# A graph layer on one core: later copies of counts and chunk sums, 560 counted chunks in passes of 30 units, four sets of one-hots

## The chip, the cores and the metric

The kernel runs on one core of a Trainium2 chip. The metric is the device time of one execution in microseconds (us). Engines are named as the profile names them: PE (TensorE, the matmuls), PEld (its weight loads), DVE (VectorE), ACT (ScalarE), POOL (GpSimd, here the issuer of gathers) and SP (SyncE, here an issuer of transfers).

## The reference

```python
h = jnp.maximum(_layernorm(x, axis=-1), 0.0)          # x: 12500 nodes x 128
xs = h[src]                                           # 200,000 edges, sorted by dst
for i in range(4):                                    # four types of edge
    msgs = msgs + jnp.where((edge_type == i)[:, None], xs @ W[i] + b[i], 0.0)
out = x + jax.ops.segment_sum(msgs, dst, num_segments=12500)
```

The edges are drawn so that low node numbers get many of them: node 0 and its neighbours are the target of very many edges, the last nodes of few.

## The kernel before, in words

First the normalized table h is written to DRAM (htab), each number in three 16-bit parts (one f16, two bf16), 384 values a row. The 200,000 sorted edges are cut into 1563 chunks of 128. They are dealt with in two ways.

**Counted chunks.** The first C0 = 568 chunks lead to the nodes with many edges. For these the kernel does not fetch rows. It counts, for each target node, how often each pair of source node and edge type occurs, and multiplies the counts with the whole table. Up to three target nodes share one 32-bit number, one byte each; such a packed group is a *unit*. The edges of a unit lie in one or more *slots* of up to 128 edges. `count` (from L1030) makes two one-hots per slot on DVE: o2 (128x392, L1049) and o1 (128x128, L1057). One matmul per slot (L1075) adds their product to the unit's bank of PSUM, `pt`, of which the pool `x_ps` has four. After the unit's last slot ACT copies the bank as integers into `counts` (L1081). The one-hots are made in sets of SLOTS = 4 slots. There are SETS = 3 sets of buffers: a set's buffers are written again when the set three before has been counted, and the loop (L1062 to L1069) keeps two sets made or in the making ahead of the one that is counted. The same pool `x_ps` also serves a bank for the weights of a group (`pc`, L646), the transposes of the results (`leave`, L750, called by `put_out`), those of the preparation (`prep_steps`) and the product with W (L1190).

A batch is up to UB = 31 units; there are 19 batches, the first of 22 units and 18 of 31, thus 580 units in 1069 slots. `multiply` (L1112 on) takes a counted batch through all 98 blocks of 128 table rows, fetched three blocks at a time (hs, 288 KB, SP). For each block PE does two matmuls (L1172) into one bank `pa`: the f16 part with the counts read as fp8 digits, and the second part in fp32r with digits that ACT has decoded (`dec`, L1130, three blocks at a time, 128 x 3 x 372, DECS = 4 buffers; three of them are decoded when the batch starts). The first batch does three fp8 matmuls instead and writes a table of two parts (dtab) for the rest. At the end ACT copies `pa` out (sd, L1186), `tail` multiplies it with W (L1190), and DVE adds it up (L1209).

After a batch has been counted, `check_sums` (L1086 to L1106) looks on DVE whether the sums hold. Its first step, `bi` (L1089), reads the last row of all counts of the batch, so it needs the batch's last copy. It is a list of steps of which the main loop takes one per part (L1508).

**Gathered chunks.** The other 995 chunks go in groups of 16 (the last groups have 8, 12, 8, 4 and 3, so 65 groups). POOL gathers one row of htab per edge (hm, L589, two chunks to a buffer, ten buffers). DVE makes one-hots of the target window (oh, L607). `sum_up` does three matmuls per chunk (L625) into `ps`, a pool `s_ps` of two banks of four chunks (SG = 4); after four chunks ACT moves the sums out (sb, L631). `weigh` brings the sums times W into `py` (L653, L655), `ring_adds` adds them to a ring (L718), and the results leave by `put_out`. The first RAW = 3 groups are read from x itself, 48 gathers of L573.

**Order.** On PE, DVE and ACT instructions run in the order in which the program emits them. The main loop (L1476 on) goes through the groups; `sum_up` hands back after each part of two chunks, and then the loop takes as much of the counted side as `pace` (L1222) says. `dense_work` (L1237) yields in turn steps of `count` of the next batch and of `multiply` of the last, by columns, with a lead of BEHIND = 0.15 for the counting, so that the counting of a batch ends before the product of the one before does. From group FULL-1 = 59 on, `pace` wants all counted work done; what is left then is 35 gathered chunks (8, 12, 8, 4 and 3), the tail. The program's one wait on the counted side between batches is by data: the first decodes (L1130) of a batch stand on ACT right behind the sd of the batch before, and the copies of the next batch's counts behind them.

Of the kernel before, what the change touches and what calls it, by code (L numbers as in the profile page):

```python
# [35 lines left out]
F32 = mybir.dt.float32  # L36
# [7 lines left out]
AF = mybir.ActivationFunctionType  # L44
# [6 lines left out]
P = 128  # L51
EPS = 1e-5
UN = 3
G = 16
SG = 4
WIN = 32
ROOM = 6
C0 = 568
UB = 31
MANY = 16  # L60
HB = 3
SLOTS = 4
ODDS = 5
SETS = 3
STREAM = 5
BEHIND = 0.15
SETTLE = 0.5
RING = 1024
OT = 4
HG = 2  # L70
# [12 lines left out]
def kernel(  # L83
# [26 lines left out]
    BM = -(-TM // P)  # L110
    BR = 16
    BC = -(-TM // BR)
    assert C0 % 8 == 0 and C0 <= NFULL


    q = E0 / E
# [226 lines left out]
    def prep_steps(m, prep):  # L343
# [22 lines left out]
        nc.vector.tensor_sub(ends[:, m : m + 1, 0], ends[:, m : m + 1, 0], span[:, m : m + 1])  # L366
        nc.vector.tensor_reduce(ends[:, m : m + 1, 1], rel, AX.X, ALU.min)
        yield 1
        pg = x_ps.tile([P, 2, P], F32, name="pt")
        nc.tensor.transpose(pg[:, 0, :], sf[:, 0, :], ident)  # L370
        nc.tensor.transpose(pg[:, 1, :], key[:, 0, :], ident)
# [229 lines left out]
    def one_hots_of(t0, g):  # L601
# [6 lines left out]

        return oh, [lambda i=i: make(i) for i in range(g)]

    adds = []
    finish = []
    flushing = []

    def sum_up(t0, g, rows, oh, last):
        win = window_of(C0 + t0)
        K = NT * win
        sb = []
        finish.append(weigh(t0, g, oh, sb, last))
        for i0 in range(0, g, SG):  # L620
            i1 = min(i0 + SG, g)
            ps = s_ps.tile([P, 512], F32, name="ps")[:, : SG * K].rearrange("p (i n) -> p i n", i=SG)
            for i in range(i0, i1):
                for c in range(3):
                    nc.tensor.matmul(ps[:, i - i0, :], rows(i, c), oh[:, i, :], start=(c == 0), stop=(c == 2))  # L625
                if i % HG and i + 1 < i1:
                    yield (i + 1) / g
            if i0 == 0:
                to = spool.tile([P, G * KM], F32, name="sb", bufs=1)[:, : G * K]
                sb.append(to.rearrange("p (g t n) -> p g t n", g=G, t=NT))  # L630
            nc.scalar.activation(  # L631
                sb[0][:, i0:i1].rearrange("p g t n -> p g (t n)"), ps[:, : i1 - i0, :], AF.Copy, scale=1.0 / UP
            )
            yield i1 / g

    def weigh(t0, g, oh, sb, last):
        win = window_of(C0 + t0)

        def bank(own):
            to = y_ps.tile([P, G * WIN], F32, name="py") if own else x_ps.tile([P, G * WIN], F32, name="pt")  # L640
            return to[:, : G * win].rearrange("p (g n) -> p g n", g=G)

# [383 lines left out]
    def count(vs, counts):  # L1026
# [34 lines left out]
        made = []  # L1061
        done = 0  # L1062
        for n, of in enumerate(sets):
            while len(making) < min(n + 3, len(sets)):
                making.append(make(len(making)))
                made.append([])
            for m in range(n, min(n + 2, len(sets))):
                made[m] += list(making[m])
            for k, (i, s, by, first, last) in enumerate(of):  # L1069
                if n + 2 < len(sets) and len(made[n + 2]) < len(sets[n + 2]):  # L1070
                    made[n + 2].append(next(making[n + 2]))
                o1, o2, _ = made[n][k]
                if first:
                    pb = x_ps.tile([P, NB + NT], F32, name="pt")
# [3 lines left out]
                if k == len(of) - 1:  # L1078
                    released[before + n] = one.ins
                if last:  # L1080
                    nc.scalar.copy(counts[:, :, i * NT : (i + 1) * NT], pb.rearrange("p (b t) -> p b t", t=NT))  # L1081
                done += 1
                yield done / len(todo)
            made[n] = None

        def check_sums():  # L1086
            n = len(vs)
            bi = sdp.tile([P, UB], I32, name="bi")
            nc.vector.tensor_copy(bi[:, :n], counts[:, NW, : n * NT].rearrange("p (i t) -> p i t", t=NT)[:, :, 0])  # L1089
            yield True  # L1090
# [22 lines left out]
    def multiply(vs, counts):  # L1113
# [71 lines left out]
        sd = sdp.tile([P, 3 * UB * NT], F32, name="sd")  # L1185
        nc.scalar.activation(sd[:, :nv], pa[:, :nv], AF.Copy, scale=512.0 / UP)  # L1186
        def tail():
            py = x_ps.tile([P, 3 * UB], F32, name="pt")
            for t in range(NT):
                nc.tensor.matmul(  # L1190
# [285 lines left out]
    for gi, (t0, g) in list(enumerate(zip(starts, sizes)))[RAW:]:  # L1476
# [20 lines left out]
        for j, part in enumerate(sum_up(t0, g, *now, gi >= FULL)):  # L1497
# [204 lines left out]
```

## Time and profile before

| what | value |
|---|---|
| median of 3 runs | 1642.27 us |
| the three runs | 1640.22, 1642.27, 1651.68 us |
| the profiled execution | 1648.93 us |
| its span, first to last instruction | 1647.2 us |
| mean granted clock of PE | 0.909 of full |
| instructions | 30145 |

How to read it: in a row of groups, the line of the kernel, the engine and the operation come first, then what is written and read with its shape, the number of instructions, the busy time of all, the mean of one in ns, and the idle time of that engine just in front of them with the one that ended most of it. "issue" is a time in front of which nothing in the profile was waited for. In a row of waits the three numbers are the total in us, how many times, and the longest. In a row of the timeline stand the start, the time from first to last, the engine, the line and the operation, and in brackets the idle time before. In a row of windows stand the stretch, its length, the busy time of PE, PEld, DVE, ACT and POOL with their instruction counts, the granted clock of PE, the share of the DMA engines and GB/s.

### The profile page before, as it was taken

What the parts mean: (1) busy time and instruction counts of PE and PEld (TensorE: products, weight loads), DVE (VectorE), ACT (ScalarE), POOL (GpSimd) and SP (SyncE); (2) the same over time, 40 slices, a digit from 0 to 9 for tenths busy, and PEclk for the clock granted to TensorE, in tenths of its full rate; (3) what the DMA queues carried; (4) which work ended last, traced back from release to release, by engine and by line L of the source; (5) the groups of instructions that cost most, each with busy time, mean ns of one, the idle gap of its engine ahead of it and who ended that gap; (6) DMA issues with size and microseconds to landing.
All of it is one profiled execution on the core that took longest, in us unless ns stands there. A gap on an engine that the chain in (4) does not pass through costs nothing.

```text
span 1647.2 us, 30145 instructions
## 1 busy us (share of the span) xinstructions
PE 1345.8 (82%) x9232; PEld 902.9 (55%) x9232; DVE 999.9 (61%) x5139; ACT 1082.6 (66%) x1815; POOL 970.2 (59%) x1024
## 2 busy tenths in 40 slices
PE   4876878888888888798878879788879888797965
PEld 1344655565655555465655556555656655565644
DVE  7785559466666657666554756456554746564523
ACT  5676446676767677677767677677767767666621
POOL 6535444656656565656656665566656666656563
PEclk9785897989999898998999999999989999999977
DMA  7542695766766676767766676576767676667842
GB/s 215 168 170 67 206 335 162 237 185 205 210 190 207 185 224 176 217 186 211 210 196 208 205 214 203 172 215 199 211 186 213 190 220 197 191 177 219 254 120 75
DMA packets 184628, 322.54 MB, mean 196 GB/s; under 512 B 30243, under 2 KB 82524, under 8 KB 184460
## 3 DMA queue, kind: packets, MB, share of 16 engines
q1 hardware_dynamic: 132716, 214.63, 42.1%
q0 software_dynamic: 46992, 96.30, 20.9%
q10 hardware_dynamic: 4752, 9.64, 1.5%
q8 instruction: 73, 1.20, 0.3%
q14 instruction: 95, 0.78, 0.1%
HBM read 294.78 MB, written 25.67 MB: 195 GB/s over the span
## 4 chain that ended last, share of the span: by engine, by line
PE 65%; issue 11%; ACT 9%; DVE 8%; DMA 3%; another core or an unknown queue 3%; POOL 0%; SPq 0%; DVEq 0%; ACTq 0%
PE pa L1172 33%; PE pt L1075 12%; PE py L655 7%; PE ps L625 6%; ACT dec L1130 4%; DVE o L1057 2%; DVE o L1049 2%; PE pt L1190 2%; DVE ring L718 1%; ACT counts L1081 1%; DMA hs<-htab 1%; DMA hs<-dtab 1%; PE pt L646 1%; PE pt L936 1%
## 5 line engine op out<-in xcount | busy, mean ns | idle before, releaser
L589 POOL DMA_INDIRECT hm<-htab,srcT x947 | 918.0, 969 | 616.8 <-issue 217.2
L1130 ACT ACTIVATE dec<-counts 128x1116 fp32r<-128x1116 uint8 (+1 forms) x594 | 663.2, 1137 | 23.9 <-remote 13.7
L1049 DVE TENSOR_SCALAR o<-iota_n,hkT 128x392 bf16<-128x392 f16 x1069 | 351.8, 329 | 300.6 <-PE pt L1075 172.9
L1172 PE MATMUL pa<-dec,hs 128*128 128x372 f32 x1764 | 498.5, 389 | 30.6 <-issue 19.8
L1172 PE MATMUL pa<-counts,hs 128*128 128x372 fp8e4 (+1 forms) x2058 | 449.7, 330 | 48.0 <-issue 22.8
L1075 PE MATMUL pt<-o,o 128*128 128x396 bf16 x1069 | 308.9, 359 | 98.0 <-issue 37.7
L1172 PEld LDWEIGHTS pa<-dec,hs 128*128 128x128 f32 x1764 | 317.9, 195 | 99.5 <-issue 44.3
L1081 ACT CAST counts<-pt 128x396 int32<-128x396 f32 x580 | 272.5, 496 | 148.2 <-PE pt L1075 55.7
L1172 PEld LDWEIGHTS <-hs 128*128 128x128 f16 (+1 forms) x2058 | 191.1, 99 | 191.7 <-issue 73.2
L631 ACT ACTIVATE sb<-ps 128x288 f32<-128x288 f32 (+8 forms) x237 | 98.3, 415 | 238.6 <-PE ps L625 76.0
L1057 DVE TENSOR_SCALAR o<-iota,loT,byT 128x128 bf16<-128x128 bf16 x647 | 213.8, 330 | 0.0
L625 PE MATMUL ps<-oh,hm 128*128 128x72 bf16 (+7 forms) x2841 | 185.8, 202 | 32.7 <-issue 25.9
L625 PEld LDWEIGHTS <-hm 128*128 128x128 f16 x2841 | 139.2, 101 | 97.6 <-issue 54.1
L718 DVE TENSOR_TENSOR ring<-ring,py 128x18 f32 (+6 forms) x912 | 158.5, 174 | 55.5 <-issue 21.5
L607 DVE TENSOR_SCALAR oh<-iota_b,keyT 128x72 bf16<-128x72 bf16 (+7 forms) x947 | 164.0, 259 | 39.0 <-PE ps L625 20.7
L1075 PEld LDWEIGHTS <-o 128*128 128x128 bf16 x1069 | 83.0, 102 | 150.6 <-issue 96.6
L655 PE MATMUL py<-sb,wsb 128*128 128x288 f32 (+6 forms) x456 | 131.7, 435 | 9.7 <-issue 8.6
L1057 DVE TENSOR_SCALAR o<-iota,loT 128x128 bf16<-128x128 bf16 x422 | 118.0, 280 | 0.0
L655 PEld LDWEIGHTS py<-sb,wsb 128*128 128x128 f32 x456 | 87.7, 204 | 47.8 <-issue 20.5
L1089 DVE COPY bi<-counts 128x31 int32<-128x31 int32 (+1 forms) x19 | 5.0, 261 | 132.7 <-issue 84.2
L573 POOL DMA_INDIRECT hx<-in_x_dram,srcT x48 | 47.0, 978 | 38.5 <-DVE sel L887 13.1
L650 ACT CAST cnt<-pt 128x288 bf16<-128x288 f32 (+10 forms) x62 | 24.4, 394 | 31.1 <-PE ps L625 9.4
(250 smaller groups left out, 777.6 us busy)
## 6 DMA issues: line engine op xcount, KB each, us to landing
hs<-dtab SPq DMA_DIRECT2D x576, 288.0 KB
hm<-htab,srcT POOLq DMA_INDIRECT x947
htab<-h SPq DMA_DIRECT2D x32, 288.0 KB
hs<-htab SPq DMA_DIRECT2D x32, 288.0 KB
dtab<-dec ACTq DMA_DIRECT2D x32, 288.0 KB
xo<-in_x_dram SPq DMA_DIRECT2D x23, 256.0 KB
out_dram<-xo SPq DMA_DIRECT2D x23, 256.0 KB
hm<-in_x_dram SPq DMA_DIRECT2D x18, 192.0 KB
```

Of the source, the lines that this page charges most:

```text
L589: one = nc.gpsimd.indirect_dma_start(out=hm[:, (i - h0) * D3 : (i - h0 + 1) * D3], out_offset=None, in_=htab, in_offset=bass.IndirectOffse ...
L607: nc.vector.tensor_scalar(oh[:, i, :], iota_b[:, :K], keyf[:, at : at + 1], None, ALU.is_equal)
L625: nc.tensor.matmul(ps[:, i - i0, :], rows(i, c), oh[:, i, :], start=(c == 0), stop=(c == 2))
L631: nc.scalar.activation(sb[0][:, i0:i1].rearrange("p g t n -> p g (t n)"), ps[:, : i1 - i0, :], AF.Copy, scale=1.0 / UP)
L655: nc.tensor.matmul(py[:, :g, :], wsb[:, t, :], sb[0][:, :g, t, :], start=False, stop=(t == NT - 1))
L718: nc.vector.tensor_tensor(to, to, of(i), ALU.add)
L1049: one = nc.vector.tensor_scalar(o2[:, k, :NB], iota_n, hkT[:, s : s + 1], None, ALU.is_equal)
L1057: one = nc.vector.tensor_scalar(o1[:, k], iota_1, loT[:, s : s + 1], by, ALU.is_equal, ALU.mult)
L1075: one = nc.tensor.matmul(pb, o1, o2, start=first, stop=last)
L1081: nc.scalar.copy(counts[:, :, i * NT : (i + 1) * NT], pb.rearrange("p (b t) -> p b t", t=NT))
L1130: nc.scalar.activation(decoded[n][:, : j1 - j0, :nv].rearrange("p j (m v) -> p j m v", m=3), by_digit[:, j0:j1, : nu * NT * 4].rearrange(" ...
L1172: nc.tensor.matmul(to if c == 1 and not first else to.rearrange("p (m v) -> p m v", m=3), left, right, start=(j == 0 and c == 0), stop=(js ...
```

## The change

Five things, with the diff below.

1. C0 goes from 568 to 560 and UB from 31 to 30. There are again 19 batches: 24 units and 18 x 30, thus 564 units in 1053 slots; the matmuls of L1172 have 360 columns (288 in the first batch) where they had 372 (264). 1003 chunks are gathered in 65 groups: 61 of 16, then 12, 8, 4 and 3. The counted work is now to be done by group 60, with 27 gathered chunks left.
2. SETS goes from 3 to 4, and sets of one-hots are made three ahead of the one counted, not two.
3. The copy of a unit's counts (L1081) is not emitted at once but kept in a list, `owed`. It is emitted after the last matmul of the next unit, or earlier, when something else takes a bank of `x_ps` (preparation, weights, results, `tail`), and at the end of the batch.
4. The eviction of four chunk sums (L631) is kept in `sums_owed` and emitted when the next block of four begins, before the steps of the raw groups, or before the last group's end.
5. `check_sums` first lets REST_PARTS = 6 parts pass.

```diff
-C0 = 568
-UB = 31
+C0 = 560
+UB = 30
...
-SETS = 3
+SETS = 4
...
+REST_PARTS = 6
...
+    owed = []
+    sums_owed = []
+
+    def settle(of):
+        while of:
+            of.pop(0)()
...
     def sum_up(t0, g, rows, oh, last):
...
+        def evict(i0, i1, ps):
+            if i0 == 0:
+                to = spool.tile([P, G * KM], F32, name="sb", bufs=1)[:, : G * K]
+                sb.append(to.rearrange("p (g t n) -> p g t n", g=G, t=NT))
+            nc.scalar.activation(
+                sb[0][:, i0:i1].rearrange("p g t n -> p g (t n)"), ps[:, : i1 - i0, :], AF.Copy, scale=1.0 / UP
+            )
+
         for i0 in range(0, g, SG):
             i1 = min(i0 + SG, g)
+            settle(sums_owed)
             ps = s_ps.tile([P, 512], F32, name="ps")[:, : SG * K].rearrange("p (i n) -> p i n", i=SG)
...
+            sums_owed.append(lambda i0=i0, i1=i1, ps=ps: evict(i0, i1, ps))
             yield i1 / g
...
         def bank(own):
+            settle(owed)
...
-            while len(making) < min(n + 3, len(sets)):
+            while len(making) < min(n + SETS, len(sets)):
                 making.append(make(len(making)))
                 made.append([])
-            for m in range(n, min(n + 2, len(sets))):
+            for m in range(n, min(n + SETS - 1, len(sets))):
                 made[m] += list(making[m])
             for k, (i, s, by, first, last) in enumerate(of):
-                if n + 2 < len(sets) and len(made[n + 2]) < len(sets[n + 2]):
-                    made[n + 2].append(next(making[n + 2]))
+                m = n + SETS - 1
+                if m < len(sets) and len(made[m]) < len(sets[m]):
+                    made[m].append(next(making[m]))
...
                 if last:
-                    nc.scalar.copy(counts[:, :, i * NT : (i + 1) * NT], pb.rearrange("p (b t) -> p b t", t=NT))
+                    settle(owed)
+                    owed.append(
+                        lambda i=i, pb=pb: nc.scalar.copy(
+                            counts[:, :, i * NT : (i + 1) * NT], pb.rearrange("p (b t) -> p b t", t=NT)
+                        )
+                    )
                 done += 1
-                yield done / len(todo)
+                if done < len(todo):
+                    yield done / len(todo)
             made[n] = None
+        settle(owed)
+        yield 1.0
 
         def check_sums():
             n = len(vs)
+            for _ in range(REST_PARTS):
+                yield True
...
         def tail():
+            settle(owed)
...
                 if raw_steps:
+                    settle(sums_owed)
                     raw_steps.pop(0)()
...
             assert not ending and not flushing and not soon
+            settle(sums_owed)
             next(finish.pop(0))
```

`settle(owed)` stands also ahead of the transposes of `prep_steps` and of `leave`.

More of the change, by code (lines that the diff above doesn't have):

```diff
@@ L112 @@
     BC = -(-TM // BR)
-    assert C0 % 8 == 0 and C0 <= NFULL
+    assert C0 % 16 == 0 and C0 <= NFULL
     q = E0 / E
@@ L627, in sum_up @@
                     yield (i + 1) / g
[L628 to L633, printed above, removed]
+            sums_owed.append(lambda i0=i0, i1=i1, ps=ps: evict(i0, i1, ps))
             yield i1 / g
@@ L1080, in count @@
                 if last:
-                    nc.scalar.copy(counts[:, :, i * NT : (i + 1) * NT], pb.rearrange("p (b t) -> p b t", t=NT))
+                    settle(owed)
[4 more added lines that the diff above has]
+                    )
                 done += 1
-                yield done / len(todo)
+                if done < len(todo):
+                    yield done / len(todo)
             made[n] = None
+        settle(owed)
+        yield 1.0
         def check_sums():
             n = len(vs)
+            for _ in range(REST_PARTS):
+                yield True
             bi = sdp.tile([P, UB], I32, name="bi")
@@ L1187, in tail @@
         def tail():
+            settle(owed)
             py = x_ps.tile([P, 3 * UB], F32, name="pt")
```

## The prediction

> **What bounds the kernel now.** I read the page first, from top to bottom, then the waits, then the timeline and the clock around the ends of the batches, and last the tail.
>
> ```profile
> span 1647.2 us, 30145 instructions
> ...
> PE 1345.8 (82%) x9232; PEld 902.9 (55%) x9232; DVE 999.9 (61%) x5139; ACT 1082.6 (66%) x1815; POOL 970.2 (59%) x1024
> ...
> PE 65%; issue 11%; ACT 9%; DVE 8%; DMA 3%; another core or an unknown queue 3%; POOL 0%; SPq 0%; DVEq 0%; ACTq 0%
> PE pa L1172 33%; PE pt L1075 12%; PE py L655 7%; PE ps L625 6%; ACT dec L1130 4%; DVE o L1057 2%; DVE o L1049 2%; PE pt L1190 2%; DVE ring L718 1%; ACT counts L1081 1%; DMA hs<-htab 1%; DMA hs<-dtab 1%; PE pt L646 1%; PE pt L936 1%
> ...
> L589 POOL DMA_INDIRECT hm<-htab,srcT x947 | 918.0, 969 | 616.8 <-issue 217.2
> L1130 ACT ACTIVATE dec<-counts 128x1116 fp32r<-128x1116 uint8 (+1 forms) x594 | 663.2, 1137 | 23.9 <-remote 13.7
> ...
> L1172 PE MATMUL pa<-dec,hs 128*128 128x372 f32 x1764 | 498.5, 389 | 30.6 <-issue 19.8
> L1172 PE MATMUL pa<-counts,hs 128*128 128x372 fp8e4 (+1 forms) x2058 | 449.7, 330 | 48.0 <-issue 22.8
> L1075 PE MATMUL pt<-o,o 128*128 128x396 bf16 x1069 | 308.9, 359 | 98.0 <-issue 37.7
> ...
> L1081 ACT CAST counts<-pt 128x396 int32<-128x396 f32 x580 | 272.5, 496 | 148.2 <-PE pt L1075 55.7
> ...
> L625 PE MATMUL ps<-oh,hm 128*128 128x72 bf16 (+7 forms) x2841 | 185.8, 202 | 32.7 <-issue 25.9
> ...
> L655 PE MATMUL py<-sb,wsb 128*128 128x288 f32 (+6 forms) x456 | 131.7, 435 | 9.7 <-issue 8.6
> ...
> L1089 DVE COPY bi<-counts 128x31 int32<-128x31 int32 (+1 forms) x19 | 5.0, 261 | 132.7 <-issue 84.2
> ```
>
> TensorE (PE) is busy 82% of the span, and the chain that ended last runs 65% of it on PE: a third is the batch product L1172, 12% the counting L1075, 7% py L655, 6% ps L625. No other engine comes near: ACT is busy 66%, DVE 61%, and GpSimd's gathers (L589, 969 ns each) 59%, with 616.8 us of idle time. So in the long middle a change pays through the PE work that it removes, and through the times in which PE stands still. Matmul records overlap (the rows of L1172 alone sum to 948 us), so I take the chain's shares for what a matmul costs in time: L1172 0.33 x 1647.2 = 544 us, L1075 0.12 x 1647.2 = 198 us (0.185 us each), L625 99 us (0.035 us each), L655 115 us.
>
> ```profile
> DVE bi L1089 <- issue: 84.2, 10, 10.4
> ACT sb L631 <- PE ps L625: 76.0, 48, 4.7
> ...
> ACT sb L631 <- PE pt L1075: 73.1, 42, 5.5
> ...
> PEld L1075 <- DVE o L1057: 27.9, 26, 2.6
> ...
> PE pt L1075 <- ACT counts L1081: 23.2, 12, 5.2
> ...
> PEld pa L1172 <- ACT dec L1130: 19.8, 27, 2.2
> ...
> PE pt L1075 <- DVE o L1057: 14.4, 15, 2.1
> ```
>
> DVE's first step of the batch check (bi L1089) stands 84.2 us in ten waits behind a last copy of counts that isn't there yet. Behind it in DVE's order stand the one-hots of the next batch. ACT stands 149.1 us in front of sums (sb L631) that PE hasn't finished, and PE stands for one-hots (27.9 at its weight loads, 14.4 at its matmuls: largely the same stalls), for count copies (23.2) and for decoded digits (19.8).
>
> What an end of a batch looks like at its best:
>
> ```profile
> 911.15 0.65 PE L1172 MATMUL pa<-dec,hs 128*128 128x372 f32 x2
> ...
> 911.64 0.34 PE L1075 MATMUL pt<-o,o 128*128 128x396 bf16 x1
> ...
> 911.82 0.36 PE L625 MATMUL ps<-oh,hm 128*128 128x72 bf16 x6
> 911.83 0.48 ACT L1186 ACTIVATE sd<-pa 128x372 f32<-128x372 f32 x1 [1.08 <-PE pa L1172]
> ...
> 912.01 0.84 PE L1075 MATMUL pt<-o,o 128*128 128x396 bf16 x4
> ...
> 912.21 3.17 ACT L1130 ACTIVATE dec<-counts 128x1116 fp32r<-128x1116 uint8 x3
> ...
> 915.28 0.48 ACT L1081 CAST counts<-pt 128x396 int32<-128x396 f32 x1
> ...
> 915.81 0.50 PE L1075 MATMUL pt<-o,o 128*128 128x396 bf16 x2 [2.96 <-ACT counts L1081]
> ```
>
> The last product matmuls start at 911.15. ACT copies the sum out (sd), decodes three blocks for the next batch (3.17 us), and only then copies the first bank of counts, 915.28. PE has four banks for counting; it fills them and waits 2.96 us for the first to come free, though the one-hots lay ready. A less tidy end:
>
> ```profile
> 977.01 0.41 DVE L1089 COPY bi<-counts 128x31 int32<-128x31 int32 x1 [9.91 <-ACT sb L631]
> ...
> 982.06 0.68 PE L1075 MATMUL pt<-o,o 128*128 128x396 bf16 x3
> ...
> 984.19 0.41 ACT L631 ACTIVATE sb<-ps 128x288 f32<-128x288 f32 x1 [5.46 <-PE pt L1075]
> ...
> 984.49 0.47 ACT L1186 ACTIVATE sd<-pa 128x372 f32<-128x372 f32 x1
> 984.85 3.18 ACT L1130 ACTIVATE dec<-counts 128x1116 fp32r<-128x1116 uint8 x3
> ...
> 987.92 2.27 ACT L1081 CAST counts<-pt 128x396 int32<-128x396 f32 x5
> ...
> 988.46 1.15 PE L1075 MATMUL pt<-o,o 128*128 128x396 bf16 x3 [5.19 <-ACT counts L1081]
> ```
>
> Here bi waited 9.91 us, ACT then stood in an sb until 984.19, and PE waited 5.19 us. The clock around the first of the two:
>
> ```profile
> 912.00:916.00 4.00, 1.04 (x12) 0.52 (x9) 2.52 (x11) 4.00 (x7) 3.09 (x4) 1.00 0.96 343
> 916.00:920.00 4.00, 3.81 (x16) 3.07 (x15) 3.31 (x14) 2.65 (x6) 1.22 (x2) 0.57 0.31 81
> 920.00:924.00 4.00, 4.00 (x36) 2.88 (x35) 2.85 (x21) 2.85 (x4) 2.56 (x3) 1.00 0.81 223
> ```
>
> PE is busy 1.04 of the 4 us with the stall, and the granted clock, the column behind the engines, is 0.57 in the next 4 us; then 1.00 again. The stall thus costs its own length and some 0.43 x 4 = 1.7 us more.
>
> **The change part by part.**
>
> *560 chunks, batches of 30.* There are 580 units before (22 + 18 x 31) and 564 after (24 + 18 x 30), still in 19 batches. Batch products keep their count and lose width: 372 columns become 360 in the later batches, 264 become 288 in the first; in all 564/580, or 2.76% less. 544 x 0.0276 = -15.0; with the waits for operands inside those rows the saving could be nothing, or, by the busy sum, 948 x 0.0276 = 26. I take -16. Counting: 1069 slots become 1053, 16 x 0.185 = -3.0. ACT's decodes get 1080 elements for 1116 (at most 663 x 36/1116 = 21 us), its copies 16 x 0.496 = 8 us less; both lie beside PE, so nothing.
>
> Eight chunks move to the gather side (995 to 1003): 8 more gathers, some 1.3 us each, on a POOL with 617 us of idle, nothing. Because the groups become 61 full ones with the same short ones behind, counting now ends against group 60 with 27 chunks to go, where it was 35. So 16 more chunks are summed beside the counting: each costs 3 x 0.035 on L625 and 115/995 = 0.12 on L655, 0.22 in all, +3.5. And the tail loses 8 chunks. In it the gathers run like this:
>
> ```profile
> L589 POOL DMA_INDIRECT hm<-htab,srcT x34 | 32.1, 945 | 17.1 <-issue 9.1 <-remote 4.8 <-PE pt L646 2.9
> ```
>
> 34 gathers take 32.1 + 17.1 us, 1.45 each, so 8 fewer are worth 11.6 us where gathers pace the tail; bounded by 8 x 0.22 = 2 from below. The tail's POOL is nearly unbroken, so I take -10. Three fewer SP transfers and one more set of one-hots in SBUF: nothing, other work covers them.
>
> *The check six parts later.* bi no longer stands in front of the one-hots when the last copy is late, and *four sets of one-hots, made three ahead,* put 12 slots of one-hots before PE where 8 were. What goes is PE's wait for one-hots; at most 27.9 + 14.4 = 42 us, at least nothing, where PE would only arrive earlier at the bank that waits behind the decodes. Most of these waits lie near batch ends, where this is so: I take -8. Late next is ACT.
>
> *Copies of counts and sums issued later.* A copy goes out after the next unit's last matmul, an eviction at the next block of four chunks. ACT then waits less for PE, and what is behind these waits on ACT (sd, decodes) starts earlier. At the ends of batches the built order of the changed kernel still has sd, at some ends an sb, then three decodes, then the first copy; PE has, between the last product and the matmul that needs the first freed bank, mostly five to nine counting matmuls and six of ps. That is the same 1.0 to 1.4 us as in the quoted end, against the same 3.9 us of ACT (911.83 to 915.76). So 2.96 us is about the floor there, and what can be won per end lies between nothing and 5.19 - 2.96 = 2.2 us; over 17 ends 0 to 38. I take 0.5 each, nearer the tidy end since ACT sets both: -8. Since stalls of this size stay, the half clock stays at most ends; at stake is 17 x 1.7 = 29 us, and I take -3. Waits for decodes: -3 of 19.8.
>
> The price: the copy that frees a bank starts later by the next unit's matmuls, 1053/564 = 1.9 of them or 0.35 us, with at times a product block (1 us) between. The 148.2 us that ACT now stands before its copies, 0.26 us each, come off that. With four banks, and three others to fill meanwhile, most of the remainder is covered by those units' matmuls. If the cover were gone everywhere, 564 x (0.35 - 0.26) = 51 us even without product blocks; it can't gain. I take +5. The evictions of ps come later too: there are two banks of ps, and py comes only after the group's last eviction. Beside it lie counting and product matmuls; I cost that at nothing, and if the cover were gone, 65 groups would wait 0.4 us (an eviction) each, 26 us.
>
> The sum: -16 - 3 + 3.5 - 10 - 8 - 8 - 3 - 3 + 5 = -42.5. Against the profiled execution's own time, 1648.93 us, that is 1606.4; that execution stood 6.66 above the median of the three runs, 1642.27, so the median goes to about **1600 us**.
>
> **Rivals.**
>
> *Only the work and the tail pay* (1617 us). The batch ends stay as long as they are, since sd, three decodes and a copy on ACT set them (the tidy end above is all ACT), and earlier one-hots only make PE wait sooner: -16 - 3 + 3.5 - 10 = -25.5. Against it: the untidy end has 2.2 us that ACT's chain does not need.
>
> *The half clock goes* (1574 us). If the stalls shrink a little more, so that the stretch behind them keeps its clock, the whole 29 us come and not 3: -42.5 - 26 = -68.5. Against it: 2.96 us was enough to lose the clock, and the same ACT work stands there. The Trainium skill, page "TensorE: Matmul & The Clock Gate", section "What's actually happening", has the rate halved after an idle window of some 3.4 us in a free-running count, so by it a stall below 3 us should mostly be free; the trace shows a half-rate stretch after 2.96 us with 1.04 us of work in the 4, so it doesn't bear that out fully, and by the page alone the time would be this rival's.
>
> *Banks come back too late* (1665 us, slower). Late copies make four banks work like three: PE reaches the reused bank before the copy is out, above all in stretches where counting runs unbroken. With the product blocks between, a copy is later by up to 1.1 - 0.26 = 0.8 us; if one copy in four (141, those with the least work before reuse) loses 0.5 us, that is 70 us for my +5: -42.5 - 5 + 70 = +22. It decides from 0.33 us per such copy, where the 47.5 us of the rest are used up. For it: the wait for count copies is there already, 23.2 us. Against it: only in 12 places, with up to 5.2 us, thus at batch ends.
>
> *Nothing to see* (1635 us): products that shrink by 3% arrive at the same decodes and transfers, and only the tail pays, -10.
>
> **How the numbers follow.** A measurement of this kernel can tell about 1% (16 us) from no change. Chances: the forecast 0.42 (its own range 1585 to 1612), work and tail only 0.22 (1612 to 1628), half clock gone 0.12 (1555 to 1585), nothing to see 0.08 (1628 to 1650), banks late 0.16 (1645 up). Faster than 1625.8 is the first three less a sixth of the second that spills over: 0.73. Slower than 1658.7 is the late banks, less a part of them that ends between: 0.14. The rest, 0.13, is within 1%. The range that leaves out 2 in 10 cuts off the lowest part of the third case and most of the late banks: 1565 to 1648.
>
> **What would show it.** Right: L1172's rows keep their counts and lose about 3% of their mean; bi's idle time falls from 132.7 us to under 30; PE's waits for one-hots at L1075 fall to a third; at batch ends PE still waits 2.5 to 4 us for the count copies with the clock near 0.57 behind; ACT's waits for ps and pt shrink; the time behind the end of the counting is some 10 us shorter. Wrong: waits of PE for count copies in many places, not twelve, would be the late banks; full clock behind batch ends, the third case; a py that waits for sb in most groups, a price that I took as nothing.

## The result, and the profile after

The changed kernel takes 1652.26 us (median of 20 runs, 1640.73 to 1662.64), the kernel before 1646.70 (20 runs, 1631.02 to 1655.63): ratio 1.0043, 95% interval 1.0022 to 1.0064. So it is no faster; it is 0.4% slower, which is little, but the interval leaves out 1. The forecast was 1600 us in a range of 1565 to 1648.

The page of the changed kernel (line 1172 of before is 1199 now, 1075 is 1092, 1057 is 1073, 1130 is 1157, 1081 is 1100, 1089 is 1116, 1186 is 1213, 631 is 634, 625 is 644, 655 is 670, 646 is 661, 589 is 591):

```profile
span 1653.9 us, 30420 instructions
...
PE 1330.4 (80%) x9240; PEld 908.8 (55%) x9240; DVE 997.3 (60%) x5123; ACT 1059.3 (64%) x1801; POOL 975.3 (59%) x1032
...
PE 65%; issue 10%; ACT 10%; DVE 7%; DMA 4%; another core or an unknown queue 4%; DVEq 0%; SPq 0%; ACTq 0%
...
L591 POOL DMA_INDIRECT hm<-htab,srcT x955 | 923.5, 967 | 615.1 <-issue 217.3
L1157 ACT ACTIVATE dec<-counts 128x1080 fp32r<-128x1080 uint8 (+1 forms) x594 | 644.7, 1103 | 205.8 <-PE pt L1092 60.1
...
L1199 PE MATMUL pa<-dec,hs 128*128 128x360 f32 x1764 | 488.2, 383 | 29.2 <-issue 25.9
L1199 PE MATMUL pa<-counts,hs 128*128 128x360 fp8e4 (+1 forms) x2058 | 448.4, 329 | 48.9 <-issue 38.8
L1092 PE MATMUL pt<-o,o 128*128 128x396 bf16 x1053 | 297.9, 353 | 93.2 <-issue 39.4
...
L1100 ACT CAST counts<-pt 128x396 int32<-128x396 f32 x564 | 266.5, 491 | 132.1 <-PE pt L1092 73.8
```

The products (L1199) and the counting (L1092) are shorter, if by less than planned (the products' mean by 1.5% and 0.3%, for some 3%), and PE is busy 1330 us where it was 1346. Yet the span is 6.7 us longer. The first step of the batch check, once the longest wait of DVE, costs nothing any more:

```profile
L1116 DVE COPY bi<-counts 128x30 int32<-128x30 int32 (+1 forms) x19 | 4.1, 214 | 0.0
```

What the engines wait for now:

```profile
ACT dec L1157 <- PE pt L1092: 60.1, 40, 3.8
...
ACT dec L1157 <- PE pa L1199: 51.2, 41, 3.3
...
PE pt L1092 <- ACT counts L1100: 26.3, 11, 5.8
...
PEld py L670 <- ACT sb L634: 16.6, 11, 4.3
...
PEld L1092 <- DVE o L1073: 16.2, 9, 5.1
...
PE pt L1092 <- DVE o L1073: 11.8, 5, 4.9
```

PE's waits for one-hots fell from 27.9 and 14.4 to 16.2 and 11.8, and its waits for count copies stayed (23.2 in 12 places, now 26.3 in 11). ACT's waits for PE moved from the sums to the decodes.

The middle, from the first to the last copy-out of a batch's sums (sd), in both kernels. The columns are the stretch, its length, the busy time of PE, PEld, DVE, ACT and POOL with the instruction counts, clock, DMA share, GB/s:

```profile
247.10:1579.00 1331.90, 1133.87 (x7980) 768.32 (x7980) 806.78 (x4210) 928.88 (x1416) 812.25 (x841) 0.94 0.68 202
```

```profile
249.50:1594.40 1344.90, 1117.44 (x7999) 775.77 (x7999) 806.72 (x4197) 906.64 (x1402) 817.60 (x849) 0.93 0.68 200
```

PE's busy time went from 1133.87 to 1117.44, which is -16.4. But the stretch is 13.0 us longer, so PE's time without work went from 198.0 to 227.5. Before the stretch it took 2.4 us more (249.5 for 247.1), and behind it 8.7 less (59.5 for 68.2): 2.4 + 13.0 - 8.7 = 6.7. These are one profile of each kernel, and single runs of a kernel lie up to 25 us apart. Note the last engine column: 841 and 849 gathers; 1331.9/841 and 1344.9/849 are both 1.584 us a gather.

One end of a batch in the changed kernel shows what the time without work is:

```profile
985.27 0.31 PE L661 MATMUL pt<-oh,three 128*32 128x288 bf16 x4
...
987.83 0.95 POOL L591 DMA_INDIRECT hm<-htab,srcT  x1 [0.30 <-issue]
...
989.08 0.95 POOL L591 DMA_INDIRECT hm<-htab,srcT  x1 [0.30 <-issue]
...
991.36 1.03 PE L1092 MATMUL pt<-o,o 128*128 128x396 bf16 x4 [0.39 <-PE pt L1092]
991.44 0.40 ACT L665 CAST cnt<-pt 128x288 bf16<-128x288 f32 x1 [4.86 <-PE pt L1092]
...
991.75 0.94 POOL L591 DMA_INDIRECT hm<-htab,srcT  x1 [1.73 <-PE pt L1092]
991.81 0.32 DVE L1065 TENSOR_SCALAR o<-iota_n,hkT 128x392 bf16<-128x392 f16 x1 [6.13 <-PE pt L1092]
...
992.04 0.48 ACT L1213 ACTIVATE sd<-pa 128x360 f32<-128x360 f32 x1
...
992.39 3.10 ACT L1157 ACTIVATE dec<-counts 128x1080 fp32r<-128x1080 uint8 x3
...
995.37 1.67 ACT L1100 CAST counts<-pt 128x396 int32<-128x396 f32 x4
...
995.92 0.49 PE L1092 MATMUL pt<-o,o 128*128 128x396 bf16 x1 [3.53 <-issue]
```

The four matmuls of L661 ended at 985.6. ACT stands for their result until 991.44, DVE for another one until 991.81, POOL for a free buffer until 991.75. Three engines are released within 0.4 us, by signals of PE (the changes of a semaphore by which others learn that a result is there) that were due at different times, the first almost six us ago. Up to 989.08 POOL had issued one gather after the other, 1.25 us apart; then it had to pause itself.

### The profile page after: what moved, and what is told of

The parts are those of the page before. It is cut to its first block, busy times and chain, and to the rows that moved or that the text cites. A ratio compares the mean times of both kernels' runs of the same rounds, so it can differ in the third digit from the quotient of the medians.

```text
span 1653.9 us, 30420 instructions
## 1 busy us (share of the span) xinstructions
PE 1330.4 (80%) x9240; PEld 908.8 (55%) x9240; DVE 997.3 (60%) x5123; ACT 1059.3 (64%) x1801; POOL 975.3 (59%) x1032
## 4 chain that ended last, share of the span: by engine, by line
PE 65%; issue 10%; ACT 10%; DVE 7%; DMA 4%; another core or an unknown queue 4%; DVEq 0%; SPq 0%; ACTq 0%
PE pa L1199 32%; PE pt L1092 12%; PE py L670 8%; PE ps L644 6%; ACT dec L1157 5%; DMA hs<-dtab 2%; ACT counts L1100 2%; PE pt L1218 2%; DVE ring L733 1%; DMA dtab<-dec 1%; DVE o L1073 1%; DVE o L1065 1%; PE ps L702 1%; PE pt L952 1%
## 5 line engine op out<-in xcount | busy, mean ns | idle before, releaser
L1157 ACT ACTIVATE dec<-counts 128x1080 fp32r<-128x1080 uint8 (+1 forms) x594 | 644.7, 1103 | 205.8 <-PE pt L1092 60.1
L1199 PE MATMUL pa<-dec,hs 128*128 128x360 f32 x1764 | 488.2, 383 | 29.2 <-issue 25.9
L1199 PE MATMUL pa<-counts,hs 128*128 128x360 fp8e4 (+1 forms) x2058 | 448.4, 329 | 48.9 <-issue 38.8
L1092 PE MATMUL pt<-o,o 128*128 128x396 bf16 x1053 | 297.9, 353 | 93.2 <-issue 39.4
L1199 PEld LDWEIGHTS pa<-dec,hs 128*128 128x128 f32 x1764 | 316.7, 197 | 80.6 <-issue 43.4
L1199 PEld LDWEIGHTS <-hs 128*128 128x128 f16 (+1 forms) x2058 | 191.7, 100 | 224.2 <-issue 120.8
L644 PE MATMUL ps<-oh,hm 128*128 128x56 bf16 (+7 forms) x2865 | 186.6, 202 | 33.8 <-issue 21.5
L733 DVE TENSOR_TENSOR ring<-ring,py 128x14 f32 (+6 forms) x928 | 161.8, 174 | 78.9 <-issue 20.2
L609 DVE TENSOR_SCALAR oh<-iota_b,keyT 128x56 bf16<-128x56 bf16 (+7 forms) x955 | 161.9, 258 | 74.3 <-PE ps L644 39.6
L670 PE MATMUL py<-sb,wsb 128*128 128x224 f32 (+6 forms) x464 | 142.2, 455 | 28.7 <-issue 21.8
L1092 PEld LDWEIGHTS <-o 128*128 128x128 bf16 x1053 | 81.7, 102 | 106.6 <-issue 53.9
L634 ACT ACTIVATE sb<-ps 128x224 f32<-128x224 f32 (+7 forms) x239 | 99.0, 415 | 39.8 <-PE ps L644 15.2
L665 ACT CAST cnt<-pt 128x224 bf16<-128x224 f32 (+10 forms) x62 | 24.6, 396 | 75.2 <-PE pt L1092 32.5
L1218 PE MATMUL pt<-sd,wsb 128*128 128x90 f32 (+1 forms) x152 | 34.4, 390 | 14.0 <-ACT counts L1100 7.9
```

The lines of the kernel that those rows point to most:

```text
L609: nc.vector.tensor_scalar(oh[:, i, :], iota_b[:, :K], keyf[:, at : at + 1], None, ALU.is_equal)
L634: nc.scalar.activation(sb[0][:, i0:i1].rearrange("p g t n -> p g (t n)"), ps[:, : i1 - i0, :], AF.Copy, scale=1.0 / UP)
L670: nc.tensor.matmul(py[:, :g, :], wsb[:, t, :], sb[0][:, :g, t, :], start=False, stop=(t == NT - 1))
L733: nc.vector.tensor_tensor(to, to, of(i), ALU.add)
L1092: one = nc.tensor.matmul(pb, o1, o2, start=first, stop=last)
L1157: nc.scalar.activation(decoded[n][:, : j1 - j0, :nv].rearrange("p j (m v) -> p j m v", m=3), by_digit[:, j0:j1, : nu * NT * 4].rearrange(" ...
```

## The experiments

Each session ran its kernels beside the kernel before. The sessions turned out to be of two kinds: in some the kernel before takes 1647 to 1666 us, as in the result, in the others 1372 to 1374. The expectations call that two chips. The last run came from the same chip as the first four, and was of the other kind, so it isn't the chip alone; I speak of *late* and *prompt* sessions below, for a reason that the fourth group shows. Each comparison stays within its session.

### Parts of the change (a prompt session, before 1372.65 us)

The sizes alone, in the kernel before:

```diff
-C0 = 568
-UB = 31
+C0 = 560
+UB = 30
```

> The kernel before with 560 chunks and batches of 30 alone; copies, evictions, sets and checks as before. Theory A (the later copies and evictions bring new waits of PE, which eat what the sizes save): the work and the tail pay without new waits, 22 to 28 us less than before, ratio 0.983 to 0.987; PE's waits behind count copies stay near 31 us in the middle. Rival B (the time of a batch does not follow its width: 33 blocks of fixed length and the end on ACT set it): ratio 0.997 to 1.003, PE's idle time grows by as much as its work shrinks though nothing is issued later.

Measured: 1368.58 us, ratio 0.9963 (0.9946 to 0.9980). Neither: a gain, but at most a fifth of what theory A has.

Count copies at once, in the changed kernel:

```diff
-                    owed.append(
-                        lambda i=i, pb=pb: nc.scalar.copy(
-                            counts[:, :, i * NT : (i + 1) * NT], pb.rearrange("p (b t) -> p b t", t=NT)
-                        )
-                    )
+                    nc.scalar.copy(counts[:, :, i * NT : (i + 1) * NT], pb.rearrange("p (b t) -> p b t", t=NT))
```

> The changed kernel, but each count copy is issued right behind its unit's last matmul, as before. Evictions of sums stay late, four sets and the late check stay. Theory A: the 23 us of added waits for count copies and the 12 us in front of the product with W go, 25 to 35 us less than the changed kernel, ratio to before 0.98 to 0.99. Rival B: no difference to the changed kernel, 1.002 to 1.006.

Measured: 1370.43 us, ratio 0.9971 (0.9954 to 0.9988).

Evictions at once, in the changed kernel:

```diff
-            sums_owed.append(lambda i0=i0, i1=i1, ps=ps: evict(i0, i1, ps))
+            evict(i0, i1, ps)
```

> The changed kernel, but each eviction of chunk sums is issued right behind its matmuls, as before; count copies stay late. Theory A: the 18 us of py waiting for sums and the 5 us of ps waiting for them go, 12 to 22 us less than the changed kernel, ratio to before 0.99 to 0.997. Rival B: no difference to the changed kernel.

Measured: 1369.02 us, ratio 0.9968 (0.9950 to 0.9987). Beside the changed kernel of another prompt session, 1368.43 us (below), neither run is faster, so the 12 to 35 us of theory A don't come.

Both edits together:

> The changed kernel with copies and evictions both at once: what is left of the change are the sizes, four sets of one-hots and the late check. Theory A: the sizes' saving and the one-hot waits together, 30 to 45 us less than before, ratio 0.973 to 0.982. Rival B: 0.997 to 1.004; the one-hot waits turn into waits for the copy behind three decodes.

Measured: 1370.43 us, ratio 0.9984 (0.9962 to 1.0006). In such a session no order of issue makes a difference that can be told, and the sizes save 4 us and not 22.

### The whole, and the decodes ahead (a prompt session, before 1373.32 us)

> The kernel before, unchanged, for its profile beside the others. The first four experiments took 1364 to 1374 us and the kernel before 1373 beside them, where it took 1647 in the runs of the result, so the machine differs by chip. In e1_sizes the gathers ran at 1.27 us each from start to end, near their shortest step of 1.25, and PE was busy 95% of the middle. Theory C (on such a chip the stream of gathers and PE are both near their limit): the kernel before has pauses between its gathers there, mean step 1.29 to 1.33 us in the middle, and PE over 95% busy. Rival B (fixed length of a batch): mean step 1.27 as in e1_sizes and PE idle as there, 57 us over the batches.

> The changed kernel, unchanged, beside the parts of it. On a chip like that of the first four experiments: theory C 0.994 to 1.0, gathers back to back at 1.27 us and PE with idle time that they set. On a chip like that of the result: 1.002 to 1.007 as there.

Measured: 1371.19 us for the one look at before; 1368.43 for the changed kernel, ratio 0.9960 (0.9942 to 0.9979). The middle of both:

```profile
218.90:1303.30 1084.40, 1035.32 (x7978) 739.52 (x7979) 804.31 (x4210) 913.34 (x1415) 808.58 (x833) 0.99 0.81 248
```

```profile
219.60:1303.70 1084.10, 1019.65 (x7998) 735.87 (x7999) 801.16 (x4197) 895.17 (x1402) 811.39 (x836) 0.98 0.80 248
```

PE's busy time falls by 15.7 us again, and the length by 0.3. The kernel before has 49.1 us without work on PE, the changed one 64.5. Gathers are 1084.1/836 = 1.297 us apart, and 1.251 is the median step: there is little room left in POOL's stream. The kernel before has 1.302 and a PE that is busy 95.5% of the stretch, as theory C has it.

The late issue alone, in the sizes of before:

```diff
-C0 = 560
-UB = 30
+C0 = 568
+UB = 31
...
-SETS = 4
+SETS = 3
```

> The late copies, the late evictions and the late check alone, with the old 568 chunks and batches of 31, and three sets of one-hots since four don't fit beside 31. Theory A (late issue brings waits): 1.01 to 1.02. Theory C on a fast chip: 0.995 to 1.003, since PE's work is the old one and what the order wins or loses is small; on a slow chip as theory A.

Measured: 1371.70 us, ratio 0.9983 (0.9964 to 1.0001).

The first decodes of a batch ahead (core of the edit, in `multiply`; the following batch's counts are handed in, with a flag that is set when all are copied):

```diff
         def decode(n):
             j0, j1 = n * DS, min(n * DS + DS, NW)
-            if first or j0 >= NW:
+            if first:
+                return
+            if j0 >= NW:
+                if follow and follow[2]:
+                    ahead_of(n - -(-NW // DS), *follow[:2])
+                return
+            if n in decoded:
                 return
```

> The changed kernel, but the first three decodes of a batch are issued one by one during the last three blocks of the batch before, as soon as its counts are all copied, and not behind the copy-out of its sums. Then ACT has only that copy-out ahead of the first count copy at an end of a batch. If the three decodes set the stalls at the ends (theory of the forecast): PE's waits there fall from 2.5 to 4 us to about 1, the half clock behind them mostly goes, and on a chip like that of the result the time falls by 40 to 70 us, ratio 0.96 to 0.98. Rival C (gathers set the end): on a fast chip the ratio stays 0.99 to 1.0, the same as the changed kernel.

Measured: 1368.56 us, ratio 0.9957 (0.9941 to 0.9972): the changed kernel's time. PE's waits for count copies fall from 27.2 us in 15 places to 1.3 in 2, and PE then waits longer for rows, in the changed kernel (first) and in this one:

```profile
PE ps L644 <- DMA hm<-htab,srcT: 38.8, 52, 1.8
```

```profile
PE ps L644 <- DMA hm<-htab,srcT: 70.6, 99, 2.2
```

What is won at the ends of batches is given back in front of the sums of gathered rows, where the waits grow by 32 us.

### Half the gathers (a late session, before 1647.04 us)

These kernels leave out the rows of every second chunk: one gather fills a buffer of two chunks, and both chunks are summed from its rows. All matmuls, one-hots and copies stay.

```diff
-            for i in range(h0, min(h0 + HG, g)):
+            for i in range(h0, h0 + 1):
                 at = (t0 + i) % (TURN * P)
                 one = nc.gpsimd.indirect_dma_start(
...
-        return lambda i, c: of(got[i // HG], c)[:, (i % HG * 3 + c) * D : (i % HG * 3 + c + 1) * D]
+        return lambda i, c: of(got[i // HG], c)[:, c * D : (c + 1) * D]
```

> The kernel before, with the rows of every second chunk left out: one gather per buffer of two chunks, and both chunks are summed from its rows. All matmuls, one-hots and copies stay. Theory C (on a chip like that of the parts, the gathers pace the middle): PE's idle time of 48 us falls to 25 or less and the time is 20 to 45 us less than the kernel before, ratio 0.967 to 0.985. If PE's own work sets the time: 0.997 to 1.003. Theory H for a chip like that of the result (PE's signals to the other engines come late while a gather is in flight, 1.65 us at the median copy-out of a batch and up to 5.3, where they come after 0.04 us each time on the other chip): with half the gathers the late signals become about half as many, and the time falls by 100 us or more, ratio under 0.94.

> The changed kernel with the rows of every second chunk left out in the same way. With the gathers out of the way its smaller products should show: theory C says 16 to 25 us less than h1_before_half (the three pairs of products of a step took 0.980 us for 1.014, 20 us over all), while with all rows the changed kernel was only 5 us faster. Rival B (a batch has a fixed length): the same time as h1_before_half within 0.3%.

> The changed kernel with the first decodes of a batch issued in the last blocks of the batch before, and the rows of every second chunk left out. If the decodes behind the copy-out hold PE at the ends of batches once gathers don't pace it: 2.5 us at each of 17 ends and the slower clock behind, 40 to 70 us less than h2_after_half. If other waits stand there instead: the same as h2_after_half within 0.5%.

Measured: 1372.70 us for the kernel before with half its gathers, ratio 0.8338 (0.8311 to 0.8364); 1348.26 for the changed one, 0.8195 (0.8165 to 0.8224); 1302.52 with the decodes ahead, 0.7911 (0.7886 to 0.7937). All three are as the theories H, C and the forecast's picture of the ends have it. Their middles, in this order:

```profile
234.70:1317.90 1083.20, 1038.24 (x7979) 743.05 (x7979) 790.99 (x4208) 913.44 (x1415) 403.98 (x421) 0.98 0.70 210
```

```profile
235.00:1296.70 1061.70, 1014.03 (x7999) 735.20 (x7999) 789.73 (x4197) 893.93 (x1402) 411.45 (x426) 0.98 0.71 215
```

```profile
236.10:1251.80 1015.70, 1003.06 (x7999) 729.69 (x7999) 785.55 (x4197) 892.23 (x1402) 411.39 (x426) 0.99 0.74 224
```

PE's time without work is 45.0, 47.7 and 12.6 us, where it was 198.0 and 227.5 with all rows in the session of the result. The first stretch is as long as that of the kernel before with all rows in a prompt session (1084.40), the second is 22.4 us shorter than that of the changed kernel there (1084.10): in prompt sessions PE paces the one, the gathers the other. Now the smaller products show: 24.4 us less (1372.70 to 1348.26). And the waits of PE for count copies, in the second and the third of them:

```profile
PE pt L1092 <- ACT counts L1100: 28.3, 13, 3.1
```

```profile
PE pt L1092 <- ACT counts L1100: 3.7, 6, 1.8
```

Twelve of the 13 places lie 3.9 to 4.2 us behind a copy-out: the ends of batches, as the forecast had them. Without the three decodes in front of the copy they go, and 45.7 us with them.

Why this is about late signals: the copy-out (sd, L1186) needs the last product (L1172). Ahead of 14 of the 19 copy-outs in the profile of before ACT stands idle, and these waits are put down to

```profile
  PE pt L1075: 18.2, 5
  remote: 3.8, 1
  PE ps L625: 3.4, 3
  PE pa L1172: 3.1, 4
```

The name is that of the last signalling instruction that had ended by then. Only 4 times is it the product; the 8 matmuls of L1075 and L625 all ended after the last product, so its signal came when younger results were there too. (At the other five copy-outs ACT was held in an earlier instruction.) One of them:

```profile
1128.21 0.64 PE L1172 MATMUL pa<-dec,hs 128*128 128x372 f32 x2
...
1134.01 0.48 ACT L1186 ACTIVATE sd<-pa 128x372 f32<-128x372 f32 x1 [5.42 <-PE pt L1075]
```

The product ended at 1128.85, and ACT stood until 1134.01 with nothing before the copy-out. In the prompt session the same kernel has

```profile
  PE pa L1172: 31.4, 19
```

and from the rows, the copy-out starts 0.04 us behind the end of the last product at every one of the 18 ends that follow the first. In the profile of before the 18 delays are 0.04 to 5.34 us, median 1.65, in the changed kernel's 2.5. With half the gathers, in the same kind of session, they are 0.04 again in 16 of 18.

The traces also hold the times at which PE's semaphore changed. At the end of a batch shown above it changes at 987.06, then not until 991.36, and then seven times in 0.38 us: as many as signalling matmuls ended from 985.59 to 990.97. Over the whole middle of before, in the 1.25 us behind the start of a gather, signalling matmuls end at 1.3 per us and the semaphore changes 0.6 times per us; when the last gather started 2 to 3 us ago, 1.0 matmuls end per us and it changes 7.5 times. In the prompt session it is 1.5 for 1.5 in those first 1.25 us. So in a late session PE's signals are held while gathers follow one another, and come through when POOL pauses. Half the gathers make fewer of them late, not none: 409 of PE's 1971 signals have no recorded change within 0.3 us of the matmul's end, where it is 1251 with all rows and 23 in the prompt session (some changes are missing from the record: it has 1478, 1752 and 1935 of them).

The gathers themselves are not slower in a late session. Their queue in before (first, 1647.2 us) and in the prompt session's profile of the same kernel (1369.5 us):

```profile
q0 software_dynamic: 46992, 96.30, 20.9%
```

```profile
q0 software_dynamic: 46992, 96.30, 25.3%
```

That is 344 and 346 us, the mean of the 16 DMA engines, for the same packets, and the median step from gather to gather is 1.25 us in both.

A caution on the late profiles: they record fewer changes of semaphores (12347 in before, 19223 with half the gathers, 35039 in the prompt session). Who ended a wait is inferred from these, so in late rows the names, and what stands under "issue", are less sure than the times. The 84.2 us of bi under "issue" in before, for one, have a name in the prompt session:

```profile
DVE bi L1089 <- ACT counts L1081: 91.3, 17, 8.1
```

### The parts once more

These runs repeat parts in two more sessions, both prompt (before 1374.41 and 1371.85 us).

> 560 chunks and batches of 30 alone, as e1_sizes. On a chip like that of the result: if the later issue is what eats the saving (theory A), 0.983 to 0.990; if the eight more gathers with the signals that they hold eat it (theory H), 0.998 to 1.004. On the other chip 0.996 as in e1_sizes.

> The late copies, evictions and checks alone with 568 chunks and batches of 31, as s1_schedule. On a chip like that of the result: theory A 1.012 to 1.02, theory H 0.995 to 1.006. On the other chip 0.998 as in s1_schedule.

> The changed kernel with the first decodes of a batch in the last blocks of the batch before, with all rows gathered, as d1_decodes_ahead. On a chip like that of the result: if the ends of batches cost what they cost with half the gathers (46 us), ratio 0.972 to 0.982; if PE only waits elsewhere for late signals, 0.998 to 1.006. On the other chip 0.996 as in d1_decodes_ahead.

> The changed kernel with copies and evictions issued at once: sizes, four sets and the late check, as e4_both_at_once. On a chip like that of the result: theory A 0.975 to 0.988, theory H 0.998 to 1.006. On the other chip 0.998 as in e4_both_at_once.

> 560 chunks and batches of 30 alone, as e1_sizes and p1_sizes. On a chip like that of the result: if the later issue is what eats the saving (theory A), 0.983 to 0.990; if late signals of PE eat it whatever is issued when (theory H), 0.998 to 1.004. On the other chip 0.996.

> The changed kernel with the first decodes of a batch in the last blocks of the batch before, all rows gathered, as d1_decodes_ahead and p3_decodes_ahead. On a chip like that of the result: if the ends of batches cost what they cost with half the gathers (46 us), ratio 0.972 to 0.982; if PE only waits elsewhere for late signals, 0.998 to 1.006. On the other chip 0.996.

Measured: p1 0.9959 (0.9936 to 0.9983), p2 0.9987 (0.9961 to 1.0012), p3 0.9957 (0.9936 to 0.9979), p4 0.9962 (0.9941 to 0.9983), q1 0.9973 (0.9954 to 0.9992), q3 0.9958 (0.9938 to 0.9979). The same as the first time, and nothing new on late sessions.

The last run met one (before 1666.15 us, on the chip of the first four):

> The changed kernel with copies and evictions issued at once: sizes, four sets and the late check, as e4_both_at_once and p4_both_at_once. On a chip like that of the result: theory A (late issue eats the saving) 0.975 to 0.988, theory H (late signals eat it whatever is issued when) 0.998 to 1.006. On the other chip 0.996 to 0.998.

Measured: 1671.04 us, ratio 1.0016 (0.9993 to 1.0039). That is theory H: with copies and evictions at once the sizes, the four sets and the late check save nothing there either. Its middle:

```profile
254.70:1610.80 1356.10, 1127.48 (x7999) 772.97 (x7999) 806.84 (x4197) 906.15 (x1402) 817.97 (x849) 0.93 0.67 199
```

849 gathers in 1356.1 us, 1.597 us each; PE has 228.6 us without work, as in the changed kernel. Theory A falls. A gather's 1.597 us, for 1.584 in the session of the result, goes with a kernel before that is 1.2% slower here, so this step isn't a constant. Whether the late issue adds anything isn't settled: 1.0043 (1.0022 to 1.0064) and 1.0016 (0.9993 to 1.0039) overlap.

## Why the prediction was wrong

*The work: right as a sum.* -16 for products, -3 for counting and +3.5 for 16 more chunks beside the counting make -15.5; PE's busy time in the middle fell by 16.4 us, in a prompt session by 15.7, and with half the gathers by 24.2. Term by term it isn't shown: the products' means fell by 1.5% and 0.3%, not by some 3%.

*The tail: right in the kind of session that was forecast from.* -10 was taken, -8.7 came. In a prompt session it is -2.4 (66.2 to 63.8 us), since there 43 gathers are left behind the last copy-out before and 40 after, where it is 35 and 27 in the late ones.

*The check and the one-hots: half right, and nothing in the time.* bi's idle time went to 0.0. Of 42.3 us of waits for one-hots 28.0 are left, where a third was to be left, and the 14.3 us gone are not in the span.

*The ends of batches: right as a picture, at the wrong time.* PE still waits there behind three decodes, as the forecast held; that this is worth 46 us was shown where gathers are out of the way. In the changed kernel's own profile the copy-out comes 2.5 us late at the median (1.65 before), and the end shown above has PE waiting 3.53 us.

*The clock: as the row said.* Behind that end, too, the clock is lower: PE worked 0.47 of the 4 us from 992, and was granted 0.50 in the next 4:

```profile
988.00:992.00 4.00, 1.90 (x13) 0.80 (x13) 0.19 (x1) 0.56 (x2) 1.97 (x3) 1.00 0.54 151
992.00:996.00 4.00, 0.47 (x3) 0.18 (x2) 3.83 (x18) 4.00 (x7) 3.09 (x4) 0.70 0.82 275
996.00:1000.00 4.00, 4.00 (x21) 3.50 (x21) 0.11 (x2) 3.72 (x7) 0.59 (x1) 0.50 0.31 75
```

So the half clock stayed. The rule of the Trainium skill, "TensorE: Matmul & The Clock Gate", section "What's actually happening" (half rate after an idle window of about 3.4 us), doesn't fit this end as it stands: a granted 0.70 from 992 to 996 is half rate for 2.4 of the 4 us, from 993.6 on, only some 1.2 us after PE's last matmul ended at 992.39. In the 3.4 us before that PE had worked 1.6 us, so here a window with much idle time was enough.

*The step that failed:* "8 more gathers, some 1.3 us each, on a POOL with 617 us of idle, nothing", and with it that in the long middle PE's work is what a change pays through. In a late session the idle time of POOL is no room. PE's signals are held while its gathers run, the engines that wait for PE stand, PE then stands for them, and POOL too, for buffers that PE has read. So PE's 198 us without work hung on the gathers: with half of them 45 are left, and 274 us of the time go, in a session of the same kind. The forecast took those 198 us as separate waits, each with its own remedy, and expected the removed work and the removed waits to shorten the span. In place of the removed work PE has 29.5 us more without work. The step from gather to gather was 1.584 us in the middle before and after; the eight additional gathers there at that step are 12.7 us, and the stretch grew by 13.0. That the two agree to 0.3 us is partly luck, with single runs 25 us apart. Shown is that the gathers make this idle time, and that the smaller products pay 24.4 us once half the gathers are gone; that eight more cost 12.7 us is a reading, since no late session had another number of gathers with all else the same but the halved one.

*In a prompt session another limit stands there.* Gathers come at 1.30 us for a shortest of 1.25, so saved work turns into waits for rows.

*The rivals:* The time, 1652.26 us, lies in the range of "Banks come back too late" (1645 up), but its cause didn't come: PE waits for count copies in 11 places, and in 15 in the prompt session, not in 141. "Nothing to see" (1635; its own -10 would make it 1632) has the right outcome, that only the tail pays, and not the cause; that the middle grew it didn't have. The weight loads of py wait 16.6 us for sums in 11 places, where the price was taken as nothing; with copies and evictions at once (r4) it is 8.8 us in 4, and the span is not clearly shorter for it.

What stays open: what makes a session late, and which part of a gather holds the signals, its issue on POOL or its transfers, since half the gathers halves both. Each change of a semaphore is also written into the profile, and no run tells whether that writing has a part in the delay. The sizes alone, and the late issue alone, met no late session. One of the 35 runs of before in the first prompt session took 1765.58 us, and nothing here tells why. The Trainium skill, "Perfetto Trace Analysis", section "DMA Instruction — SWDGE (GPSIMD)", says that the profiled end of such an instruction is the end of writing descriptors, not of the transfer, so the 0.95 us rows of POOL don't tell how long a gather is in flight; no run here shows it. And the decodes ahead with all rows were only run in prompt sessions, where they gain nothing over the changed kernel.

## What to carry to other kernels

Idle time ahead of an engine's instruction is room only if it is known what the engine waits for, and whether that wait is itself made by this engine. Before the waits of a busy engine are costed one by one, look whether several engines are released at the same instant by results of different age: then look for one common cause first; here neither the removed work nor the removed waits paid while it was there. And a cheap way to see what work is worth is to take half of a suspected stream away and time both kernels again.

## What the runs showed of the hardware

In prompt sessions the copy-out starts 0.04 us after the end of the matmul that it needs, at each of 18 ends; in late ones, of the same kernel and once on the same chip, 0.04 to 5.34 us after it, and the kernel takes 1647 to 1666 us for 1372. In the late profile of before PE's semaphore changes 0.6 times per us in the 1.25 us behind a gather's start, where 1.3 signals are due, and 7.5 times per us when POOL has started none for 2 to 3 us. With every second gather left out the kernel takes 1372.70 us in such a session, as in a prompt one.
